# Heads' buffers, tied blocks, an early table load and layer 1's order on POOL and ACT: a two-layer kernel on one Trainium2 core

## The chip, the core and the metric

The kernel runs on one core of a Trainium2 chip. The core has five engines that run side by side, each in the order of its own queue: PE multiplies matrices (its weight loads are shown apart as PEld), DVE (VectorE) and ACT (ScalarE) work on elements, POOL (GpSimd) does slower element work, and SP (SyncE) here issues the DMAs, 16 DMA engines moving the data. On-chip memory has 128 partitions; sums of matmuls lie in the banks of PSUM, everything else in SBUF. Matmul operands of type fp32r are made in pairs, a high part and the low remainder, and three matmuls replace one exact product.

The metric is device time in microseconds (us), the median of several runs. A profile shows one execution. Its times run from the start of its span. A value in the form `out<-in` names the tiles by the program's names.

## The reference, cut

Two layers run over x of shape (4, 512, 1024). Each layer is an attention part and a feed-forward part, both on a layer-normalised x, both added to x.

```python
x = L0_attn_x
x = x + _L0_attn_ref(_layernorm(x, axis=-1))
x = x + _L0_ffn_ref(_layernorm(x, axis=-1), L0_ffn_W_base, ...)
x = x + _L1_attn_ref(_layernorm(x, axis=-1), L1_attn_wq_a, ...)
x = x + _L1_ffn_ref(_layernorm(x, axis=-1), L1_ffn_W, ...)
...
# _L1_attn_ref: 32 heads, 512 positions, causal
scores = jnp.einsum('bqhd,bkhd->bhqk', q_full, k_full) * softmax_scale
scores = jnp.where(causal[None, None], scores, jnp.finfo(scores.dtype).min)
attn = jax.nn.softmax(scores, axis=-1)
out = jnp.einsum('bhqk,bkhd->bqhd', attn, v).reshape(B, S, H * VD)
return out @ wo.T
...
# _L1_ffn_ref
q = x_q.mean(axis=1)                      # positions 179 to 510
routing = jax.nn.softmax(q @ router_W.T + router_b, axis=-1)
base = x @ W.T + b
t = jnp.einsum('bsd,erd->bser', x, A)
lora = jnp.einsum('bser,eor,be->bso', t, B, routing) * SCALING
return base + lora
```

The change lies in the second layer alone.

## The kernel before

The rows of x are 16 tiles of 128, four per batch. The second layer's attention runs in three stages.

*Projections* (`project`, `keep`, pools named `c1_...`). Tile after tile, PE sums the query and key projections into the bank `pq` (three banks), ACT takes the squares and the square root of the norm, and scales `qn`. PE transposes into `pn` (two banks), from there ACT and DVE write `qT` and `kT` in two halves, and SP stores them in DRAM (`q_d`, `kT_d`, `kF_d`, `k_d`). Beside the last tiles, `query` makes the queries of heads 0 and 1 in the bank `po` of pool `c1_pw`; `rotate_query` (ACT copies to `qf`, DVE makes `t`, POOL multiplies and adds) and `split_query` (DVE `qh`, POOL `ql`) follow.

*Heads* (pools `c2_...`). The units are group g of eight heads, batch b, head i. For each unit `scores` makes four rows of scores in the two banks of `pss`; for each row a custom DVE instruction (L874) adds the causal mask, writes `p` and takes the minimum, and ACT's Exp (L877) makes it probabilities. `turn` transposes p through `pst` (L898, copies at L900), `context` (L914) multiplies by v, and `divisors` sends the reciprocals of the sums through DRAM (`r_d`, then `rb`, one buffer) to the other partitions. `query` for unit u + 2 goes through the one bank `psq`. Fillers run between: `prepare_output` makes a group's output weights from `woT` and `wv` (`fetch_output` loads them into `slotC`) in eight blocks of two matmuls (`block`, L1022), each followed by ACT copies (`kept`, `high`) and DVE subtractions (`low`, `less`); `project` at L963 multiplies a finished batch by them and adds it to x in the tiles `xs` (pool `c2_x`, five buffers), loaded from and stored to `x_d` in DRAM. In these stages the order of each engine is made by a scheduler from priorities and its own estimate of times; `tc.issue_after(ins)` holds work back behind an instruction in that order. A pool stacks its tiles in memory where a closed pool's lay, so that a first write waits for the last use of what lay there, stores included.

*Layer 1's feed-forward part* (from `manual_schedule` on: PE, DVE, ACT and POOL keep the order of the program text; SP's order is the scheduler's). First the last batch's projection, 14 steps over two pairs of tiles; `fetch_last(j)` loads its four `xs` of the pair that starts at tile j. Then eight pairs of tiles, q = 0 to 7. Each pair is made in seven products (`STEPS`: b11, t1, t2, b22, t3, b21, t4), each in two halves s of the weights, with operands `ah` (ACT) and `al` (POOL) that are split ahead in three buffers. Weights come by `load_w1`: halves `wb`, `wt` or in the slots A, B, C; the kinds b11, b22 and b21 are partly split on the chip by `split_w1`. `product(q, step, s)` issues 12 matmuls and DVE adds the bank to the pair's tile (L1464; named `xo` for odd q, `raw` for even q). POOL adds the bias a quarter tile at a time (`biased`, L1442). Once per batch the routing is computed (`mixture`); `weighed` goes on in three moves through `go_on`: DVE weighs the LoRA inputs, then PE transposes them and ACT copies `hwh`, then DVE makes `hwl`; `lora` then multiplies and adds. `norm(q + 1, t)` normalises the next pair's tile t on ACT with `off` from `scales` on DVE, and `turn1` transposes it. `hs` holds these tiles; `wk` (`d_work`) holds small ones.

The pair's small tiles of LoRA are those of pair q - 1: for odd q, `weighed` is begun at step 2, copied at the end of step 3 and finished in step 4, where `lora(q - 1, 0)` follows; for even q it runs in steps 0 and 1. Pairs 2b and 2b + 1 belong to batch b, and the routing of a batch is computed at step 6 of its even pair, when the odd pair's tiles have been transposed. So an odd q has `lora` of the even pair of its own batch, an even q from 2 on (`behind`) that of the odd pair of the batch before.

The line that matters most for the wait at the junction:

```python
to = p[:, OF[i] : OF[i] + n]
turn_of[0] = V.tensor_tensor_reduce(out=to, in0=ps[:, 0:n], in1=causal[:, S - n : S], scale=1.0,
```

Of the kernel before, what the change touches and what calls it, by code (L numbers as in the profile page):

```python
# [46 lines left out]
def block_kernel(ctx: ExitStack, tc: tile.TileContext, a: dict, out: bass.AP):  # L47
# [662 lines left out]
    with tc.tile_pool(name="c1_w", bufs=1, side="right") as wap, \  # L710
            tc.tile_pool(name="c1_work", bufs=2) as wk, \
            tc.tile_pool(name="c1_pt", bufs=2, space=PSUM) as ptp, \
            tc.tile_pool(name="c1_pq", bufs=3, space=PSUM) as pqp, \
            tc.tile_pool(name="c1_pn", bufs=2, space=PSUM) as pnp, \
            tc.tile_pool(name="c1_pw", bufs=1, space=PSUM) as pwp:
        for ch in range(1, ND):
            split_shared(wap, ch)

# [9 lines left out]
        def project(s, hts):  # L728
            hh, hl = hts
            pq = pqp.tile([P, NA], F32, name="pq")  # L730
            for ch in range(ND):
                matmul3(pq, hh[:, ch, :], hl[:, ch, :], wA[ch][0], wA[ch][1],
                        start=(ch == 0), stop=(ch == ND - 1))
            j = order1[s] % TPB
            ss = small.tile([P, 2], F32, name="ss")
            junk = wk.tile([P, QR], F32, name="junk")
            A.activation(junk, pq[:, 0:QR], AF.Square, scale=QR ** -0.5, accum_out=ss[:, 0:1])
            A.activation(junk[:, 0:KVR], pq[:, QR : QR + KVR], AF.Square, scale=KVR ** -0.5,
                         accum_out=ss[:, 1:2])
            rs = rsqrt(ss, 2, 1e-6)  # L740
            qn = wk.tile([P, QR], F32, name="qn")
            kf = wk.tile([P, P], F32, name="kf")
            A.mul(qn, pq[:, 0:QR], rs[:, 0:1])
            V.scalar_tensor_tensor(out=kf[:, 0:KVR], in0=pq[:, QR : QR + KVR],
                                   scalar=rs[:, 1:2], in1=kvlnw, op0=ALU.mult, op1=ALU.mult)
            pe = QR + KVR
            half = ROPE // 2
            t1 = wk.tile([P, ROPE], F32, name="kt1")
            V.tensor_tensor(t1, pq[:, pe : pe + ROPE], ropeN[:, 0, j, :], ALU.mult)
            t2 = wk.tile([P, ROPE], F32, name="kt2")  # L750
            V.tensor_tensor(t2[:, 0:half], pq[:, pe + half : pe + ROPE],
                            ropeN[:, 1, j, 0:half], ALU.mult)
            V.tensor_tensor(t2[:, half:ROPE], pq[:, pe : pe + half],
                            ropeN[:, 1, j, half:ROPE], ALU.mult)
            V.tensor_tensor(kf[:, KVR:P], t1, t2, ALU.add)
            return qn, kf
# [22 lines left out]
                A.copy(kF, pn[:, 2, :])  # L779
                nc.sync.dma_start(out=kF_d[b], in_=kF)  # L780

        hts, qk = hts1, {}
        stats1[TPB - 1] = statistics([x[:, t, :] for t in order[-NB:]], "c", 4)
        for s in range(NT + 1):
            if s < NT:
                qk[s] = project(s, hts[s])
            if s + 2 < NT:
                hts[s + 2] = turn1(s + 2, ptp)
            if s > 0:
                keep(s - 1, qk[s - 1])  # L790
                if order1[s - 1] == TPB - 1:
                    batches[0, 0] = load_batch(0, 0)
            if s in (6, 10):
                wq_raw = fetch_query(s // 4 - 1)
            if s in (8, 12):
                wqs[s // 4 - 2] = prepare_query(wq_raw, pwp)
            if s in (NT - 2, NT - 1):
                query(s - NT + 2, pwp, "po")
                rotate_query(s - NT + 2)
            if s == NT - 1:  # L800
                split_query(0)
    c1.close()
    xpool.__exit__(None, None, None)

# [2 lines left out]
    with ExitStack() as c2:  # L807
# [3 lines left out]
        pso = c2.enter_context(tc.tile_pool(name="c2_pso", bufs=1, space=PSUM, side="right"))  # L811
        heads = c2.enter_context(ExitStack())
        tp = heads.enter_context(tc.tile_pool(name="c2_t", bufs=3))
        pp = heads.enter_context(tc.tile_pool(name="c2_p", bufs=2))
        rdp = heads.enter_context(tc.tile_pool(name="c2_rd", bufs=1))
        rdd = heads.enter_context(tc.tile_pool(name="c2_rdd", bufs=4, space=DRAM))
# [4 lines left out]

        OF = {3: 0, 2: 512, 1: 896, 0: 1152}

        sums_of = [None]

        turn_of = [None]
# [6 lines left out]
        def divisors(u, rs2):  # L833


            ri = turned_in[u // 2 % 2]
            V.reciprocal(ri[:, 0 : 2 * TPB], rs2.rearrange("p h i -> p (h i)"))
            rt = rdp.tile([P, 32], F32, name="rt")
            V.transpose(rt, ri)
            r_d = rdd.tile([2, TPB, P], F32, name="r_d")  # L840
            for k in range(P // 32):
                at = slice(k * 32, (k + 1) * 32)
                nc.sync.dma_start(out=r_d[:, :, at].rearrange("h i t -> (h i) t"),
                                  in_=rt[k * 32 : k * 32 + 2 * TPB, :])
            rb = divided[u - 1] = rdp.tile([P, S], F32, name="rb")
            for k in range(2):
                nc.sync.dma_start(out=rb[k * KVR : (k + 1) * KVR, :],
                                  in_=r_d[k].rearrange("i t -> (i t)").partition_broadcast(KVR))
# [4 lines left out]
        def scores(u):  # L853
# [10 lines left out]
            for i in range(TPB - 1, -1, -1):  # L864
                n = (i + 1) * P
                ps = pss.tile([P, S], F32, name="pss")
                if i == 0:
                    T.matmul(ps[:, 0:n], lhsT=f[:, 0:P], rhs=kF, start=True, stop=True)
                else:
                    at = slice((i - 1) * P, i * P)  # L870
                    matmul3(ps[:, 0:n], h[:, at], l[:, at], kT[:, 0, 0:n], kT[:, 1, 0:n],
                            start=True, stop=True)
                to = p[:, OF[i] : OF[i] + n]
                turn_of[0] = V.tensor_tensor_reduce(out=to, in0=ps[:, 0:n], in1=causal[:, S - n : S], scale=1.0,  # L874
                                                    scalar=-NEG, op0=ALU.add, op1=ALU.min,
                                                    accum_out=mn[:, i : i + 1])
                A.activation(to, to, AF.Exp, bias=mn[:, i : i + 1], scale=-1.0,  # L877
                             accum_out=rs[:, i : i + 1])
                if i > 0:
                    yield  # L880
# [126 lines left out]
        def prepare_output(g, fetched):  # L1007
# [9 lines left out]
            def block(n, half, at):  # L1017
                nonlocal fetched
                wo, wv = fetched
                po[at] = pso.tile([P, 512], F32, name="po" + at)  # L1020
                for k in range(2):
                    T.matmul(po[at][k * KVR : (k + 1) * KVR, :], lhsT=wv[:, k, :],  # L1022
                             rhs=wo[k][:, half * 512 : half * 512 + 512], start=True, stop=True)
                if half and n + 1 < len(prs):
                    fetched = fetch_output(g, prs[n + 1])

# [199 lines left out]
        abp = dp.enter_context(tc.tile_pool(name="d_a", bufs=1))  # L1226
        splits = dp.enter_context(tc.tile_pool(name="d_split", bufs=3))
        ptp = dp.enter_context(tc.tile_pool(name="d_pt", bufs=2, space=PSUM))
        NP = NT // 2
        blocks, sums, roots, offs = {}, {}, {}, {}  # L1230

# [77 lines left out]
        def fetch_last(j):  # L1309
            for t, k in ((0, 0), (1, 1), (0, 1), (1, 0)):  # L1310
                at[j + t, k] = x_d[(NB - 1) * TPB + j + t][k]
                xs[j + t, k] = xsp.tile([P, 512], F32, name="xs")
                nc.sync.dma_start(out=xs[j + t, k], in_=at[j + t, k])

        fetch_last(0)
# [4 lines left out]
        for n in range(14):  # L1320
# [36 lines left out]
                pair_sums(n - 10)  # L1357
            if n in (11, 12):
                parts.append(next(ops))
    w1p += [dp.enter_context(tc.tile_pool(name="d_w1", bufs=1, side="right"))]  # L1360
    hp = dp.enter_context(tc.tile_pool(name="d_h", bufs=1))
    w1r = dp.enter_context(tc.tile_pool(name="d_c", bufs=1, side="right"))
    xop = dp.enter_context(tc.tile_pool(name="d_x", bufs=1, side="right"))
    wk = dp.enter_context(tc.tile_pool(name="d_work", bufs=2, side="right"))
    acc = dp.enter_context(tc.tile_pool(name="d_acc", bufs=1, space=PSUM))
    lop = dp.enter_context(tc.tile_pool(name="d_lo", bufs=2, space=PSUM))
    for kind in ("b11", "b22", "b21", "t1"):
# [109 lines left out]
    for step in range(7):  # L1477
# [2 lines left out]
            split_w1("b11", 1, ((0, 1), (2, 3))[step - 3], V)  # L1480
        if step > 4:
            split_w1("b22", 1, (step - 5,), V)
    mix, at_work = None, {}

    def go_on(*keys):
# [3 lines left out]
    for q in range(NP):  # L1489
# [4 lines left out]
        for step in range(7):  # L1494
# [24 lines left out]
            if more and q + 1 >= TPB // 2:  # L1519
# [8 lines left out]
                    mv, r = root(mv, 2)  # L1528
                if step == 3:
                    scales(mv, r, 2, range(2 * q + 2, 2 * q + 4))  # L1530
            if more and step in (3, 4):
                norm(q + 1, step - 3)
            if q and 1 <= step < 5:
                for n in (0, 1):
                    biased(q, 2 * step - 2 + n)
            if q == 1 and step < 4:
                for n in (0, 1):
                    biased(0, 2 * step + n)
            if q:
                product(q, step, 0, h, l)  # L1540

            if (odd and step == 4) or (behind and step == 1):
                go_on((q - 1, 0), (q - 1, 1))
            if not more and step in (5, 6):
                go_on((q, step - 5))
# [3 lines left out]
            product(q, step, 1, h, l)  # L1549
            if not more and step == 6:  # L1550
                last_out(q, 1)

            if odd and step == 0:
                next(mix)
            if (odd and step == 3) or (behind and step == 0):
                go_on((q - 1, 0), (q - 1, 1))
            if odd and step in (4, 5):
                lora(q - 1, step - 4)
            if behind and step in (1, 2):
# [101 lines left out]
```

## Time and profile before

| | |
|---|---|
| median of three runs | 1771.49 us (1770.39 to 1771.75) |
| the profiled execution's own time | 1767.69 us |
| its span | 1765.9 us, granted clock 0.997 |
| PE busy | 1716.9 us, 97% of the span |
| DVE, ACT, POOL busy | 1312.4, 901.0, 892.3 us |
| chain that ended last | PE 84%, DVE 7%, DMA 3%, ACT 2% |
| projections end, heads begin | near 423 us |
| layer 1's feed-forward part begins | near 1508 us |

PE stands on most of the chain. In a timeline row, the first number is the start in us, the second the time during which such instructions ran, then come engine, line, operation and tiles; `xN` merges N instructions, and brackets hold the idle time of the engine just before and what ended it. In a table of windows, the columns are the window, its length, the busy us of each engine with the number of instructions, the granted clock of PE (1.00 is full), the mean busy share of the DMA engines and the rate at which they moved data.

### The profile page before, as it was taken

What the parts mean: (1) busy time and instruction counts of PE and PEld (TensorE: products, weight loads), DVE (VectorE), ACT (ScalarE), POOL (GpSimd) and SP (SyncE); (2) the same over time, 40 slices, a digit from 0 to 9 for tenths busy, and PEclk for the clock granted to TensorE, in tenths of its full rate; (3) what the DMA queues carried; (4) which work ended last, traced back from release to release, by engine and by line L of the source; (5) the groups of instructions that cost most, each with busy time, mean ns of one, the idle gap of its engine ahead of it and who ended that gap; (6) DMA issues with size and microseconds to landing.
All of it is one profiled execution on the core that took longest, in us unless ns stands there. A gap on an engine that the chain in (4) does not pass through costs nothing.

```text
span 1765.9 us, 31582 instructions
## 1 busy us (share of the span) xinstructions
PE 1716.9 (97%) x10536; PEld 1432.9 (81%) x10536; DVE 1312.4 (74%) x3517; ACT 901.0 (51%) x2315; POOL 892.3 (51%) x902
## 2 busy tenths in 40 slices
PE   6999999998999999999999999999999999989999
PEld 6999999997667777767777767777767777789998
DVE  6977885776877777787777687777778777677685
ACT  7422231465765555575555575555565555443332
POOL 0553540202556565546566546566545664665554
PEclk9999999999999999999999999999999999999999
DMA  4313553345224234343333353342454233943431
GB/s 192 134 50 123 169 169 98 99 136 177 81 92 148 80 113 142 114 167 112 109 114 120 108 189 93 103 139 93 135 176 138 98 117 117 328 153 127 142 110 61
DMA packets 131939, 228.16 MB, mean 129 GB/s; under 512 B 22272, under 2 KB 58752, under 8 KB 128448
## 3 DMA queue, kind: packets, MB, share of 16 engines
q1 hardware_dynamic: 131776, 226.13, 38.1%
q8 instruction: 84, 1.38, 0.3%
q14 instruction: 79, 0.65, 0.1%
HBM read 156.60 MB, written 71.83 MB: 129 GB/s over the span
## 4 chain that ended last, share of the span: by engine, by line
PE 84%; DVE 7%; DMA 3%; ACT 2%; POOL 1%; issue 1%; SPq 0%; DVEq 0%; POOLq 0%; ACTq 0%
PE psv L914 9%; PE pst L898 7%; PE pss L143 4%; PE po L143 4%; PE po L145 4%; PE po L144 4%; PE pss L144 4%; PE pss L145 4%; PE pob L143 3%; PE poa L143 3%; PE psq L143 3%; PE psq L145 3%; PE psq L144 3%; PE pob L145 3%; PE pob L144 3%; PE poa L144 3%
## 5 line engine op out<-in xcount | busy, mean ns | idle before, releaser
L877 ACT ACTIVATE p<-p,mn 128x512 f32<-128x512 f32 (+3 forms) x512 | 284.4, 559 | 206.2 <-DVE mn L874 206.0
L697 POOL TENSOR_TENSOR qf<-qf,ropeT 64x512 f32<-64x512 f32 x128 | 165.3, 1291 | 275.8 <-ACT qf L693 274.7
L874 DVE CUSTOM_DVE_ANT_0 p<-pss,causal 128x512 f32<-128x512 f32 (+3 forms) x512 | 231.4, 486 | 32.6 <-PE pss L145 25.0
L698 POOL TENSOR_TENSOR qf<-qf,t 64x512 f32<-64x512 f32 x128 | 165.7, 1294 | 40.8 <-DVE t L696 33.0
L898 PE MATMUL pst<-ident,p 128*128 128x128 f32 x1280 | 185.1, 273 | 0.7 <-ACT pT L900 0.7
L898 PEld LDWEIGHTS pst<-ident,p 128*128 128x128 f32 x1280 | 152.9, 141 | 25.5 <-ACT pT L900 2.4
L900 ACT COPY pT<-pst 128x512 f32<-128x512 f32 x256 | 141.7, 580 | 47.8 <-PE pst L898 46.9
L706 POOL TENSOR_TENSOR ql<-qf,qh 128x384 fp32r<-128x384 f32 x128 | 129.9, 1014 | 67.0 <-DVE qh L705 64.9
L143 PE MATMUL pss<-kT,ql 128*128 128x512 f32 (+2 forms) x384 | 144.5, 376 | 4.3 <-DVE mn L874 1.6
L949 POOL TENSOR_TENSOR cxl<-s,cxh 128x256 fp32r<-128x256 f32 x128 | 96.9, 765 | 89.5 <-ACT cxh L948 61.2
L143 PE MATMUL po<-w_h,hTl 128*128 128x384 f32 (+1 forms) x384 | 133.0, 346 | 0.2 <-DVE x L398 0.2
L144 PE MATMUL pss<-kT,qh 128*128 128x512 f32 (+2 forms) x384 | 130.8, 341 | 0.0
L145 PE MATMUL pss<-kT,qh 128*128 128x512 f32 (+2 forms) x384 | 130.2, 339 | 0.0
L145 PE MATMUL po<-w_h,hTh 128*128 128x384 f32 (+1 forms) x384 | 130.1, 339 | 0.0
L144 PE MATMUL po<-w_l,hTh 128*128 128x384 f32 (+1 forms) x384 | 129.7, 338 | 0.0
L900 DVE COPY pT<-pst 128x256 f32<-128x256 f32 x128 | 54.0, 422 | 95.8 <-PE pst L898 95.4
L693 ACT COPY qf<-psq 128x512 f32<-128x512 f32 x126 | 73.9, 586 | 71.0 <-PE psq L145 70.1
L695 DVE TENSOR_TENSOR t<-psq,ropeT 32x512 f32<-32x512 f32 x126 | 87.7, 696 | 24.2 <-ACT qf L693 20.2
L143 PEld LDWEIGHTS pss<-kT,ql 128*128 128x128 f32 x384 | 72.4, 189 | 39.4 <-POOL ql L706 11.4
L877 ACT ACTIVATION_READ_ACCUMULATOR p<-p,mn 128x1 f32 x512 | 97.3, 190 | 0.0
L696 DVE TENSOR_TENSOR t<-psq,ropeT 32x512 f32<-32x512 f32 x126 | 87.1, 691 | 1.8
L991 DVE TENSOR_TENSOR xs<-xs,pob 128x512 f32<-128x512 f32 x105 | 71.2, 678 | 19.7 <-PE pob L145 19.6
(563 smaller groups left out, 4963.8 us busy)
## 6 DMA issues: line engine op xcount, KB each, us to landing
xs<-x_d SPq DMA_DIRECT2D x128, 256.0 KB
x_d<-xs SPq DMA_DIRECT2D x128, 256.0 KB
slotC<-in_woT_dram SPq DMA_DIRECT2D x32, 512.0 KB
rb<-r_d SPq DMA_DIRECT2D x128, 128.0 KB
w_t<-raw SPq DMA_DIRECT2D x32, 288.0 KB
x<-in_x_dram SPq DMA_DIRECT2D x16, 512.0 KB
x_d<-x SPq DMA_DIRECT2D x32, 256.0 KB
slotA<-q_d SPq DMA_DIRECT2D x8, 1024.0 KB
```

The costliest lines, as they stand in the source:

```text
L143: T.matmul(ps, lhsT=al, rhs=bh, start=start, stop=False, **kw)
L144: T.matmul(ps, lhsT=ah, rhs=bl, start=False, stop=False, **kw)
L145: T.matmul(ps, lhsT=ah, rhs=bh, start=False, stop=stop, **kw)
L697: G.tensor_tensor(f[mid], f[mid], ropeT[mid, 0, :], ALU.mult)
L698: G.tensor_tensor(f[mid], f[mid], t2[mid], ALU.add)
L706: G.tensor_tensor(l, f[:, P:S], f32(h), ALU.subtract)
L874: turn_of[0] = V.tensor_tensor_reduce(out=to, in0=ps[:, 0:n], in1=causal[:, S - n : S], scale=1.0, scalar=-NEG, op0=ALU.add, op1=ALU.min, ...
L877: A.activation(to, to, AF.Exp, bias=mn[:, i : i + 1], scale=-1.0, accum_out=rs[:, i : i + 1])
L898: T.transpose(ps[:, w : w + P], p[:, OF[i] + j * P : OF[i] + (j + 1) * P], ident)
L900: copy(pT[:, AT[js[0]] : AT[js[0]] + w], ps[:, 0:w])
L914: T.matmul(ps[n * KVR : (n + 1) * KVR, S - w : S], lhsT=k[:, j, :], rhs=pTs[u + n][:, AT[j] : AT[j] + w], start=(j == 0), stop=(j == TPB - 1))
L949: G.tensor_tensor(l, src, f32(h), ALU.subtract)
```

## The change

Seven edits:

1. In the projections' stage the order of the PSUM pools is changed: `c1_pw` comes ahead of `c1_pn`, and `c1_pq` last.
2. `rb` gets a pool of its own, `c2_rb`, ahead of the pool of `p`, so that `p` lies elsewhere.
3. After the last tile's scaling, ACT computes one Exp on the one-column tile `first`.
4. In group 0 the matmuls of `block` are issued behind the latest unit's last row of scores.
5. Three of the four `xs` of the last batch's first pair get a pool `d_xl`, closed after the 14 steps.
6. `d_work` is opened earlier, next to the second half of the weights.
7. In the pairs, the bias is added after the products whose sums it follows, by the table `BIASED`; in odd pairs `norm(q + 1, 0)` comes after the copy of `hwh`, and `hwl` ahead of step 4's first product.

The numbers of instructions on each engine stay, but for the one Exp. The order in SP's queue changes with it at two places: near the first blocks the loads of `slotC` come after issues of `r_d` and `rb`, and around the last batch the loads of `xs` move up, between the stores of the batch before, while the loads of `slotB` (t3) and of `wb` for b21 come later.

```diff
             tc.tile_pool(name="c1_pt", bufs=2, space=PSUM) as ptp, \
-            tc.tile_pool(name="c1_pq", bufs=3, space=PSUM) as pqp, \
+            tc.tile_pool(name="c1_pw", bufs=1, space=PSUM) as pwp, \
             tc.tile_pool(name="c1_pn", bufs=2, space=PSUM) as pnp, \
-            tc.tile_pool(name="c1_pw", bufs=1, space=PSUM) as pwp:
+            tc.tile_pool(name="c1_pq", bufs=3, space=PSUM) as pqp:
...
-            A.mul(qn, pq[:, 0:QR], rs[:, 0:1])
+            scaled[0] = A.mul(qn, pq[:, 0:QR], rs[:, 0:1])
...
             if s == NT - 1:
                 split_query(0)
+                with tc.issue_after(scaled[0].ins):
+                    A.activation(first, first, AF.Exp)
...
         tp = heads.enter_context(tc.tile_pool(name="c2_t", bufs=3))
+        rbp = heads.enter_context(tc.tile_pool(name="c2_rb", bufs=1))
         pp = heads.enter_context(tc.tile_pool(name="c2_p", bufs=2))
...
-            rb = divided[u - 1] = rdp.tile([P, S], F32, name="rb")
+            rb = divided[u - 1] = rbp.tile([P, S], F32, name="rb")
...
-                    T.matmul(ps[:, 0:n], lhsT=f[:, 0:P], rhs=kF, start=True, stop=True)
+                    scored[0] = T.matmul(ps[:, 0:n], lhsT=f[:, 0:P], rhs=kF, start=True, stop=True)
...
-                for k in range(2):
-                    T.matmul(po[at][k * KVR : (k + 1) * KVR, :], lhsT=wv[:, k, :],
-                             rhs=wo[k][:, half * 512 : half * 512 + 512], start=True, stop=True)
+                with ExitStack() if g else tc.issue_after(scored[0].ins):
+                    for k in range(2):
+                        T.matmul(po[at][k * KVR : (k + 1) * KVR, :], lhsT=wv[:, k, :],
+                                 rhs=wo[k][:, half * 512 : half * 512 + 512], start=True, stop=True)
...
+        xl = ExitStack()
+        xlp = xl.enter_context(tc.tile_pool(name="d_xl", bufs=3))
...
-                xs[j + t, k] = xsp.tile([P, 512], F32, name="xs")
+                xs[j + t, k] = (xsp if j or (t, k) == (1, 0) else xlp).tile([P, 512], F32, name="xs")
...
+    xl.close()
     w1p += [dp.enter_context(tc.tile_pool(name="d_w1", bufs=1, side="right"))]
+    wk = dp.enter_context(tc.tile_pool(name="d_work", bufs=2, side="right"))
     hp = dp.enter_context(tc.tile_pool(name="d_h", bufs=1))
     w1r = dp.enter_context(tc.tile_pool(name="d_c", bufs=1, side="right"))
     xop = dp.enter_context(tc.tile_pool(name="d_x", bufs=1, side="right"))
-    wk = dp.enter_context(tc.tile_pool(name="d_work", bufs=2, side="right"))
...
+    BIASED = {(q, step): [(q, n) for n in ns] for q in range(1, NP)
+              for step, ns in ((0, (0, 1)), (1, (4, 5)), (2, (6, 7)), (3, (2, 3)))}
+    for at, ns in (((0, 6), (0, 1)), ((1, 0), (2,)), ((1, 1), (3,)), ((1, 2), (4,)), ((1, 3), (5,)),
+                   ((1, 4), (6, 7))):
+        BIASED.setdefault(at, []).extend((0, n) for n in ns)
...
-            if more and step in (3, 4):
+            if odd and step == 4:
+                go_on((q - 1, 0), (q - 1, 1))
+            if more and step in ((4,) if odd else (3, 4)):
                 norm(q + 1, step - 3)
-            if q and 1 <= step < 5:
-                for n in (0, 1):
-                    biased(q, 2 * step - 2 + n)
-            if q == 1 and step < 4:
-                for n in (0, 1):
-                    biased(0, 2 * step + n)
             if q:
                 product(q, step, 0, h, l)
-            if (odd and step == 4) or (behind and step == 1):
+            if behind and step == 1:
                 go_on((q - 1, 0), (q - 1, 1))
...
             product(q, step, 1, h, l)
...
+            for p, n in BIASED.get((q, step), ()):
+                biased(p, n)
...
             if (odd and step == 3) or (behind and step == 0):
                 go_on((q - 1, 0), (q - 1, 1))
+            if odd and more and step == 3:
+                norm(q + 1, 0)
```

More of the change, by code (lines that the diff above doesn't have):

```diff
@@ L780, in keep @@
                 nc.sync.dma_start(out=kF_d[b], in_=kF)
-        hts, qk = hts1, {}
+        hts, qk, scaled = hts1, {}, [None]
         stats1[TPB - 1] = statistics([x[:, t, :] for t in order[-NB:]], "c", 4)
@@ L822, in block_kernel @@
         OF = {3: 0, 2: 512, 1: 896, 0: 1152}
+        scored = [None]
         sums_of = [None]
```

## The prediction

> **What bounds the kernel now.** I read the page first: PE is busy for 1716.9 us of a span of 1765.9, so only 49 us can be won at all unless PE work goes, and no PE work goes here. Then I cut the span into windows to see where those 49 us lie, and read the chain of waits, PE's waits and the timeline only there. Until 340 us PE idles 20 us, at the start, which no edit touches. The rest sits in a few places. The windows' columns are: window, length, then busy us and instructions of PE, its weight loads, DVE, ACT and POOL, the granted PE clock, the DMA share and GB/s.
>
> ```profile
> 420.00:430.00 10.00, 6.70 (x25) 3.10 (x23) 5.07 (x18) 4.32 (x11) 4.10 (x6) 0.85 0.87 279
> 430.00:440.00 10.00, 7.78 (x32) 5.84 (x32) 6.04 (x23) 7.65 (x21) 3.55 (x3) 0.81 0.50 166
> 440.00:450.00 10.00, 9.94 (x64) 7.79 (x65) 7.58 (x21) 5.84 (x16) 6.76 (x7) 1.00 0.09 27
> ...
> 1570.00:1580.00 10.00, 8.16 (x59) 7.50 (x57) 8.32 (x20) 1.89 (x4) 10.00 (x13) 1.00 0.01 2
> 1580.00:1590.00 10.00, 8.81 (x49) 7.80 (x50) 5.03 (x13) 4.23 (x8) 5.37 (x7) 0.83 0.26 96
> ```
>
> Here PE loses 5.5 us between 420 and 440 and 3.0 between 1570 and 1590, both times at a clock below 1: part of each window ran at half rate. (Between 1510 and 1570 it loses 5.3 more.) After 440 it is full. The timeline shows what it waits for at the first place, the change from projections to heads:
>
> ```profile
> 426.22 1.22 PE L1022 MATMUL poa<-slotC 128*64 128x512 f32 x4 [2.13 <-issue]
> ...
> 429.43 0.69 DVE L874 CUSTOM_DVE_ANT_0 p<-pss,causal 128x512 f32<-128x512 f32 x1 [3.31 <-DMA kT_d<-kT]
> 429.79 1.28 ACT L877 ACT_TABLE_LOAD   x1
> ...
> 440.06 0.50 PE L143 MATMUL pss<-kT,ql 128*128 128x512 f32 x1 [0.95 <-POOL ql L706]
> ```
>
> Bracketed is the idle time and what ended it. The first score row of head 0 has lain in its bank since 423.5, but DVE may not write `p` until the DMA store of the last `kT` has left that memory, at 429.4. ACT's exponentials then also wait for a table load. PE waits for the bank of `poa`, then for both score banks, at last for the third head's rotated query. The second place is layer 1's pairs with odd q:
>
> ```profile
> 1576.10 0.46 DVE L1464 TENSOR_TENSOR xo<-xo,acc 128x288 f32<-128x288 f32 x1 [1.43 <-POOL xo L1442]
> ...
> 1579.42 1.24 ACT L1266 ACTIVATE h<-h,off,y2d 128x1024 f32<-128x1024 f32 x1 [4.30 <-DVE off L1258]
> ...
> 1580.57 0.41 ACT L1432 CAST hwh<-pt 128x128 fp32r<-128x128 f32 x2
> ...
> 1581.19 0.80 PE L143 MATMUL lo<-b1h,hwl 128*128 128x512 f32 x1 [2.72 <-DVE hwl L1434]
> ...
> 1638.40 0.50 PE L143 MATMUL lo<-b1h,hwl 128*128 128x512 f32 x1 [1.14 <-DVE hwl L1434]
> ```
>
> The LoRA copy `hwh` stands on ACT behind the norm, the norm waits for `off`, and in q=1 `off` is late because a sum waited 1.43 us for POOL's bias. Lastly one wait hangs on the loads:
>
> ```profile
> 1553.76 0.38 PE L143 MATMUL acc<-wt,al 128*128 128x288 f32 x1 [1.63 <-DMA wt<-w_t]
> ```
>
> **The change, part by part. Junction at 420 to 440 (PSUM pools reordered, `rb` moved ahead of `p`, Exp loaded early, blocks tied).** In the changed program DVE's first L874 waits for PE and DVE alone. It stands behind the query scaling, which ends at 425.15 + 0.35 = 425.5 and doesn't move: ACT's table load moves into the idle 1.72 us that end at 423.37 (ACT is free from 421.65; 1.28 + 0.3 for a one-column Exp ends at 423.2). So `p` starts at 425.6, 3.8 earlier. If that cover were gone, the load would cost its 1.28 again. Follow the third head's query: four exponentials at 0.72, 0.60, 0.49, 0.39, with 0.19 each for the accumulator, end at 429.4 (from 426.4); `qf` copied at 430.0 (0.57); L695 and L696, 0.70 each, at 431.4; POOL L698 1.28 at 432.7; `qh` 0.36, `ql` 1.00 at 434.15. PE may go on at 434.2, where it did at 440.06: 5.9 earlier. The 3.8 became 5.9 because the load (1.28) and three copies of block results (1.76) no longer stand on ACT ahead of the exponentials. PE, however, owes the eight block matmuls that it did in its wait, 1.01 per four by the later rows of L1022, 2.0. I take 5.9 - 2.0 = 3.8 (rounded down). Ends: 5.9 if the owed matmuls fall into waits that remain, 2.0 if the three copies come back on the path. The tie adds a wait that PE meets anyway: blocks now stand behind head 3's scores, behind them queries and transposes. On SP the next `slotC` loads (two of 512 KB, one of 64) fall behind the `r_d` and `rb` issues; PE meets the block that needs them some 7 us of its own work later, against 2.43 and 4.11 us that the chain shows for single loads (`xs`, `raw`).
>
> [...]
>
> **LoRA copies before the norm, bias behind sums.** In q=1 the sum at 1576.10 loses its 1.43. DVE's `off` then ends near 1577.95 and step 3's sums at 1580.18 - 1.43 = 1578.75. `hwh` is copied once the transposes (1574.12 + 0.38) are there, and `hwl` now comes ahead of step 4's sums: 1579.0. PE, free at 1578.47, waits 0.6 in place of 2.72. The six LoRA matmuls cost 0.43 each at half rate against 0.23; their eight transposes then end at 1581.6, held a little by the second norm (1577.98 + 1.24 + 0.62 + 1.25), where they ended at 1585.07: 3.5. Ends: 2.1 (half rate stays), 4.0 (no wait left). For q=3 and q=5 nothing waits for POOL; `hwl` leaves the place behind the norm: DVE ends step 3's sums at 1637.39, `hwl` 0.26 later, PE starts at 1637.72 for 1638.40; the second norm takes back 0.1. Twice 0.6 is 1.2, ends 0.4 and 2.3.
>
> [...]
>
> POOL pays nothing: a bias is 0.72, a split 1.28, a step of 24 matmuls at 0.133 is 3.2. The bias now waits for DVE's sum, some 0.8 behind PE, and the next split stands behind it: 0.8 + 3 x 0.72 + 1.28 = 4.3, while that split is due two steps, 6.4, later. Beyond this margin each us would be PE's.
>
> **Last batch and small tiles.** Three `xs` buffers leave the pool of five, so loads of `x_d` no longer wait for stores. On SP four loads move up between the stores at 1505 to 1509, the other half's three also; `slotB` slides from 1503.54 behind them, and `wb` (b21, 1.18 MB) from 1511.96 behind all the `raw` loads to about 1522.5. What DVE gains (1.44 at 1526.60) hides behind POOL, busy without a break there. But the loads behind that `wb` are those that end in the 1.63. 1.18 MB at the 385 to 424 GB/s of full windows is 3.0 us, 0.65 less for the 256 KB load that left: 2.4 late at worst; of it the DMA's slack between 1520 and 1526 (shares 0.57, 0.81, 0.90 of 2 us each) takes 1.4. I take a loss of 1.0. Ends: a gain of 1.6, a loss of 2.4 and 1.3 for half rate after a 4-us gap. `d_work` moved: nothing, its first tile is written at 1536.96 after DVE idled 2.67 for PE, and `bias`, whose memory shifts, is used 28 us after its issue.
>
> **Sum.** 3.8 + 3.5 + 1.2 - 1.0 = 7.5. The profiled execution took 1767.69, 3.8 under the median of 1771.49; I apply the saving to both: 1760.2 and 1764.0.
>
> **Rivals.** (1) The junction only moves its wait: the third head's query, by way of POOL, stays where it was. Only layer 1's 3.7 remain: 1767.8. For it: that wait is a chain through four engines. Against: all of it hangs on `p`, and the new order shows no DMA there. (2) Loads decide: the b21 move costs 3.7 and the junction brings 2.0, together 3.0 saved, 1768.5. For: the DMA share is about 1.0 from 1526 to 1556. Against: the same bytes move. (3) Slower: the tied blocks become the bound. First to last block took 62 us; the first now comes near 445, 18 us later, while the first projection stays at 507 less the lead. If the block-copy-subtract chain needed all of its 62, PE would wait 18 there: 1771.5 - 7.5 + 18 = 1782; it decides once it slips by more than 7.5. Against: a block's own chain is about 3.1 us (0.5 matmul, two copies of 0.59, two subtractions of 0.69), eight are 25.
>
> **Chances.** Forecast 0.69 (its own range 1761 to 1767), rivals 0.12, 0.15 and 0.04. About 0.2%, 3.5 us, is what a measurement of this kernel tells from no change. Faster takes nearly all of the first and half of (1) and (2): 0.80; the same 0.16; slower 0.04. The terms' ends alone give 1757.7 and 1770.7; 1759.5 to 1770 leaves out under two in ten.
>
> **What would show it.** Right: L874 starts near 425.6 with no DMA as releaser, ACT's load stands before L770, PE's first wait for `ql` ends near 434; PE's waits for `hwl` fall from 5.8 to about 2.3, with the clock at 1.0 in the window after q=1. Wrong: a wait of `poa` or `pob` for `slotC` or DVE between 440 and 510, or a `wt` wait well above 1.63.

## The result, and the profile after

| | before | after |
|---|---|---|
| median | 1771.52 us (1770.39 to 1771.99, 6 runs) | 1759.94 us (1757.68 to 1762.22, 6 runs) |
| ratio, 95% interval | | 0.994 (0.9929 to 0.995) |
| the profiled execution, and its span | 1767.69, 1765.9 us | 1762.22, 1760.4 us |
| PE busy | 1716.9 us | 1714.4 us |

The kernel got faster by 11.6 us. The forecast was 7.5, 1764.0: the direction holds, and the size is half as large again. The time lies 1.1 us below the forecast's own range of 1761 to 1767 and only 0.4 us inside the wider one of 1759.5 to 1770. The two profiled executions differ by only 5.5 us, since the one of before is 3.8 under its median and the one of after 2.3 over its own. That gap is the first thing to explain.

Some windows of the profile after (window, length, then busy us and instructions of PE, its weight loads, DVE, ACT, POOL, the granted clock, DMA share, GB/s):

```profile
420.00:430.00 10.00, 7.65 (x32) 5.57 (x31) 6.91 (x27) 7.47 (x24) 5.06 (x7) 0.87 0.94 291
430.00:440.00 10.00, 9.34 (x46) 8.15 (x45) 7.07 (x20) 5.96 (x16) 5.93 (x5) 0.78 0.24 79
...
1580.00:1590.00 10.00, 10.00 (x75) 9.60 (x74) 5.28 (x11) 3.40 (x7) 5.15 (x6) 1.00 0.67 217
...
1630.00:1640.00 10.00, 10.00 (x70) 9.47 (x69) 6.81 (x19) 5.02 (x9) 5.28 (x5) 1.00 0.31 104
```

Between 420 and 440 PE idles 3.0 us in place of 5.5, yet the clock is as low as before: in this execution the half-rate stretch stayed (6.83 us from 427.48 on, 6.83 from 427.03 on in before). The windows behind q = 1 and in q = 3 are full, and the clock there is 1. The timeline of after at the junction and in q = 1:

```profile
423.06 1.28 ACT L804 ACT_TABLE_LOAD   x1
...
426.83 0.68 DVE L882 CUSTOM_DVE_ANT_0 p<-pss,causal 128x512 f32<-128x512 f32 x1
...
436.76 0.50 PE L143 MATMUL pss<-kT,ql 128*128 128x512 f32 x1 [0.66 <-POOL ql L706]
...
1574.14 0.42 ACT L1445 CAST hwh<-pt 128x128 fp32r<-128x128 f32 x2
...
1577.20 1.24 ACT L1277 ACTIVATE h<-h,off,y2d 128x1024 f32<-128x1024 f32 x1 [2.64 <-DVE off L1269]
...
1578.22 0.50 PE L143 MATMUL lo<-b1h,hwl 128*128 128x512 f32 x1 [0.87 <-DVE hwl L1447]
```

`p` no longer waits for a DMA, the table load stands ahead of it, and PE's wait for `hwl` in q = 1 fell from 2.72 to 0.87, with `hwh` copied 3 us ahead of the norm.

**How the traces are compared below.** The n-th instruction of a form (DVE's rows of scores, its sums, its reciprocals) is the same piece of work in both kernels. Its lead is how much earlier it starts than in the first profile of before; what a stretch is worth is the growth of the lead over it. Leads in us, at the time that the instruction has in the profile of before:

| profile | 420 | 538 | 1507 | 1561 | 1567 | 1607 | 1719 |
|---|---|---|---|---|---|---|---|
| after | -1.40 | 3.28 | 2.27 | 1.70 | 0.87 | 3.73 | 5.45 |
| e1, edits 1 to 4 | 0.10 | 7.19 | 6.68 | 4.63 | 4.63 | 5.98 | 5.72 |
| e2, edit 7 | -0.17 | -0.10 | -1.90 | -4.59 | -5.42 | -2.54 | -0.71 |
| e3, edits 5, 6 | 1.21 | 1.17 | 0.73 | -4.45 | -4.47 | -4.49 | -4.82 |
| e4, before again | 0.45 | 0.33 | -0.44 | -3.15 | -3.14 | -3.35 | -3.31 |
| e5, after again | 0.01 | 7.00 | 6.46 | 3.85 | 3.02 | 5.91 | 7.64 |
| e6, without 5, 6 | 0.50 | 7.14 | 6.30 | 2.68 | 1.85 | 4.73 | 6.49 |
| e7, edits 2, 5, 6 | 1.21 | 7.65 | 6.56 | 3.54 | 3.55 | 4.90 | 4.89 |
| e8, LoRA first | 0.23 | 1.78 | 1.37 | -1.87 | -1.86 | 0.19 | 1.48 |
| e9, bias moved | -0.18 | 5.36 | 4.01 | 3.37 | 3.44 | 6.21 | 7.93 |
| e10, without 3 | 1.17 | 7.22 | 6.54 | 3.48 | 2.64 | 5.54 | 7.26 |
| e11, without 4 | 1.53 | 6.23 | 5.84 | 5.42 | 4.60 | 7.50 | 9.22 |
| e12, edits 2, 7 | 1.06 | 8.26 | 7.82 | 6.33 | 6.41 | 9.24 | 11.03 |

Where a run's table of times gives a ratio, it is against the kernel before on the same chip.

### The profile page after: what moved, and what is told of

It is laid out like the page before. It is cut to its first block, busy times and chain, and to the rows that moved or that the text cites. A ratio compares the mean times of both kernels' runs of the same rounds, so it can differ in the third digit from the quotient of the medians.

```text
span 1760.4 us, 31605 instructions
## 1 busy us (share of the span) xinstructions
PE 1714.4 (97%) x10536; PEld 1433.1 (81%) x10536; DVE 1311.9 (75%) x3517; ACT 901.5 (51%) x2316; POOL 895.7 (51%) x902
## 4 chain that ended last, share of the span: by engine, by line
PE 87%; DVE 6%; DMA 3%; ACT 2%; POOL 1%; issue 1%; SPq 0%; DVEq 0%; ACTq 0%; POOLq 0%
PE psv L922 9%; PE pst L906 7%; PE po L143 4%; PE po L145 4%; PE po L144 4%; PE pss L143 4%; PE pss L144 4%; PE pss L145 4%; PE poa L143 3%; PE pob L143 3%; PE psq L143 3%; PE psq L145 3%; PE psq L144 3%; PE poa L145 3%; PE poa L144 3%; PE pob L145 3%
```

## The experiments

**The parts alone, and the kernel before again.** e1 has edits 1 to 4 of the diff, e2 edit 7, e3 edits 5 and 6, each on the kernel before; e4 is the kernel before, unchanged.

> Edits 1 to 4 alone (pool orders, the buffer of the reciprocals, the early Exp, tied blocks). By the two profiled executions the lead grows from -1.4 at 420 us to 3.3 at 510 us: 4.7 saved, so the median falls from 1771.5 to about 1766.8 (theory A: the parts add, each as large as in the traces). Theory B (the two traces miss a part, because the half-rate stretch after 427 us comes in some executions only): 7 to 8 saved, 1763.5 to 1764.5, with executions whose mean clock is 0.999 or 1.000 beside others at 0.998. My prediction's rival 1 (the wait only moves) would have 0 saved: 1771.5.

> Edit 7 alone (bias behind sums, LoRA copies ahead of the norm). By the traces q=1 saves 2.9 to 3.4 us, q=3 and q=5 0.86 each: 4.6 to 5.1 saved, 1766.4 to 1766.9 (theory A, and B too). Theory C (edit 7 counts only with the earlier loads of edits 5 and 6): under 3 saved, above 1768.5.

> Edits 5 and 6 alone (three buffers of xs apart, the small tiles' pool moved). By the traces the lead shrinks by 1.4 us between 1510 and 1567: 1.4 slower, about 1772.9 (theory A: the loads that were moved back cost this). Theory C: no loss or a small gain alone, 1770.5 to 1771.5. PE's wait for wt would be near 2.1 by A, 1.6 or less by C.

> The kernel before, once more, unchanged. Its one profiled execution took 1767.69, 3.8 under the median. Theory A: this profile was a lucky one; the new profile and the executions lie at 1770.5 to 1772, and their extra 3 to 4 us can be found in the trace in a stretch outside the edits (start to 420 us, or the heads). Theory B: the executions split into two groups by the mean clock (0.996 and 0.997 or more), and the new profile has a longer half-rate stretch near 427 or 1580 us than 7 and 5 us.

| | median, range, runs | ratio, 95% interval |
|---|---|---|
| kernel before | 1769.48 (1765.83 to 1772.59, 31) | |
| e1, edits 1 to 4 | 1762.56 (1761.21 to 1767.82, 8) | 0.9965 (0.9954 to 0.9976) |
| e2, edit 7 | 1765.20 (1763.27 to 1770.25, 12) | 0.9981 (0.9971 to 0.9991) |
| e3, edits 5, 6 | 1772.60 (1771.26 to 1774.69, 11) | 1.002 (1.0011 to 1.0028) |
| e4, before again | 1769.54 (1767.18 to 1774.05, 11) | 1.0002 (0.9993 to 1.0011) |

Edits 1 to 4 bring 6.9 us (by the interval 4.2 to 8.1), more than theory A's 4.7 and just short of B's 7 to 8. Edit 7 brings 4.3 (1.6 to 5.1), near A's 4.6. The interval alone leaves room for C, but the lead grows by 3.9 from 1561 to 1719 in e2 and by 3.8 in after, so edit 7 needs no other edit. Edits 5 and 6 alone cost 3.1 (1.9 to 5.0), twice what A had, and C's gain is out; edit 6 was never run without edit 5. The spread of the kernel before, some 7 us, is as large as what is sought, so the traces have to carry the rest. They show why it is so wide. Windows of two profiles in which the junction's code is the one of before (first e8, then e4):

```profile
430.00:440.00 10.00, 7.62 (x42) 5.86 (x41) 7.00 (x23) 6.51 (x21) 5.24 (x5) 1.00 0.43 157
```

```profile
430.00:440.00 10.00, 7.95 (x35) 6.28 (x35) 6.41 (x20) 6.69 (x20) 4.53 (x4) 0.83 0.41 155
1510.00:1520.00 10.00, 7.74 (x32) 6.28 (x31) 4.63 (x12) 6.23 (x10) 3.14 (x5) 0.83 0.83 292
```

The same waits at the junction are followed by half rate in e4 and by none in e8, whose lead grows by 1.55 from 420 to 538 with no edit in it (its window from 420 to 430 has a clock of 1.00 too). e4 has a stretch near 1517 that the first profile of before lacks. Theory B is right in this: the half-rate stretches come in some executions only. It is wrong in its groups, since times and clocks spread without two clear clusters. Theory A is right that the profile of before was a lucky one, but the place is not where A looked (before 420 us, or the heads); it is 1507 to 1561. With the loads in the order of before, six other profiles (e1, e2, e4, e6, e8, e12) lose 1.5 to 3.6 us there against it. That accounts for most of the 3.8 us to the median. Half rate is not all of it: in e2 and e12, which lose 2.7 and 1.5 there, the clock is 1.00 from 1507 to 1561, and PE's wait for `wt` is 2.7 and 2.5 us in place of 1.63.

**Why edits 5 and 6 alone lose.** SP's queue, the first sum of the last batch on DVE and PE's wait behind it in e3, by the timeline:

```profile
1504.40 4.63 SPq L995 DMA_DIRECT2D x_d<-xs  x4
1509.19 3.20 SPq L1315 DMA_DIRECT2D xs<-x_d  x7
...
1512.11 0.69 DVE L1336 TENSOR_TENSOR xs<-xs,poa 128x512 f32<-128x512 f32 x1 [3.43 <-issue]
...
1512.94 0.47 PE L143 MATMUL poa<-t20h,cxl 128*128 128x512 f32 x1 [2.43 <-DVE y L1253]
```

And SP's queue in after:

```profile
1502.88 0.33 SPq L1003 DMA_DIRECT2D x_d<-xs  x1
1503.25 0.43 SPq L1324 DMA_DIRECT2D xs<-x_d  x1
1504.25 0.32 SPq L1003 DMA_DIRECT2D x_d<-xs  x1
1504.61 0.43 SPq L1324 DMA_DIRECT2D xs<-x_d  x1
```

In e3 seven loads stand in one block behind four stores. DVE idles 3.4 us before the sum that adds to one of the loaded tiles (the view names no releaser, "issue"; the first load is issued 2.9 us before the sum starts). PE idles 2.4 until that sum has emptied the bank (the view names `y`, DVE's next instruction), after which its clock halves: matmuls on 128x512 go from 0.39 to 0.63 us. In after the loads stand between the stores. Theory D explains it by the memory that the new buffers get: without edit 2 the first of them lies where a late tile of the heads' stage lay, with `rb` in its own pool ahead of `p` it doesn't. No row shows where a tile lies, so this reason stays argued; that edits 5 and 6 hang on edit 2 can be tested.

**The full change again, without edits 5 and 6, edits 2, 5 and 6 alone, and half of edit 7.** e6 leaves out `d_xl` and the move of `d_work`. e7 takes only these and `rb`:

```diff
+        rbp = heads.enter_context(tc.tile_pool(name="c2_rb", bufs=1))
         pp = heads.enter_context(tc.tile_pool(name="c2_p", bufs=2))
...
-            rb = divided[u - 1] = rdp.tile([P, S], F32, name="rb")
+            rb = divided[u - 1] = rbp.tile([P, S], F32, name="rb")
```

e8 changes the kernel before in the pairs' order alone; the bias stays where it was:

```diff
-            if more and step in (3, 4):
+            if odd and step == 4:
+                go_on((q - 1, 0), (q - 1, 1))
+            if more and step in ((4,) if odd else (3, 4)):
                 norm(q + 1, step - 3)
...
-            if (odd and step == 4) or (behind and step == 1):
+            if behind and step == 1:
                 go_on((q - 1, 0), (q - 1, 1))
...
+            if odd and more and step == 3:
+                norm(q + 1, 0)
```

> The changed kernel once more. Against the kernel before on this chip, the three parts measured alone gave -6.9 (edits 1 to 4), -4.3 (edit 7) and +3.1 (edits 5 and 6). Theory A (parts add): -8.1, 1761.4 if the kernel before stands at 1769.5. Theory D (edits 5 and 6 cost 3.1 only where the loads of xs stand behind four stores in SP's queue; in the full change they stand between them, since edit 2 frees the memory they go to): -10.5 to -11.5, 1758 to 1759. The share of executions with clock 0.999 or 1.000 above that of the kernel before in both.

> The changed kernel without edits 5 and 6. Theory A: 3.1 faster than the full change, -11.2 against the kernel before, 1758.3. Theory D: equal to the full change within 1 us either way.

> Edits 2, 5 and 6 alone, so that the loads of xs can stand between the stores. Theory D: between 1500 and 1530 us the lead changes by less than 0.5, where edits 5 and 6 alone lost 3.2, and DVE's first sum of the last batch no longer idles 3.4; PE's wait there falls from 2.4 to 1.2 or less. Theory A: 3 lost there as before. The junction may gain or not: edit 2 moves p away from the memory of kT, so up to 4.7 saved there; if the PSUM order alone decides, 0. Time 1765 to 1770 by D, 1768 to 1773 by A.

> Half of edit 7: LoRA copies and hwl ahead of the norm, the bias where it was before. My prediction's steps: q=3 and q=5 keep their whole saving (0.6 each forecast, 0.9 measured), in q=1 PE's wait for hwl goes from 2.7 to about 1 although the sum still waits 1.43 for POOL's bias: 3.0 to 4.3 saved in all, 1765.2 to 1766.5 at 1769.5 for the kernel before. Rival: the late bias holds hwl too, because hwl stands on DVE behind the sums of step 3: only 1.8 from q=3 and q=5, 1767.7, and q=1 keeps a wait of 2 or more.

| | median, range, runs | ratio, 95% interval |
|---|---|---|
| kernel before | 1769.39 (1765.92 to 1772.03, 17) | |
| e5, the full change | 1759.10 (1755.87 to 1762.23, 6) | 0.9939 (0.9925 to 0.9953) |
| e6, without edits 5, 6 | 1758.38 (1756.44 to 1761.19, 6) | 0.9937 (0.9924 to 0.995) |
| e7, edits 2, 5, 6 | 1761.81 (1760.39 to 1764.52, 5) | 0.9956 (0.9943 to 0.997) |
| e8, LoRA first | 1767.32 (1766.18 to 1769.26, 12) | 0.9992 (0.9983 to 1.0) |

e5 and e6 are equal within the scatter, 10.3 and 11.0 saved. D had 10.5 to 11.5 for e5; A's 8.1 lies just outside its interval (8.3 to 13.3 saved), while e6 alone fits A's 11.2 as well as D. The traces decide. In e7 SP's loads stand between the stores, the lead between 1507 and 1528 shrinks by 0.14, where e3 lost 3.2, and PE waits 1.3 there for 2.4: edits 5 and 6 cost nothing there once edit 2 is in, as D says. What nobody expected is the junction in e7: 6.4 us from one moved buffer, without the other three edits.

In e8 half of edit 7 brings 2.1 us, less than the 3.0 that my step asked for. The timeline of its q = 1:

```profile
1576.89 0.43 ACT L1432 CAST hwh<-pt 128x128 fp32r<-128x128 f32 x2
...
1577.95 0.45 DVE L1464 TENSOR_TENSOR xo<-xo,acc 128x288 f32<-128x288 f32 x1 [1.43 <-POOL xo L1442]
...
1581.96 0.47 DVE L1434 TENSOR_TENSOR hwl<-pt,hwh 128x128 fp32r<-128x128 f32 x2
...
1582.30 0.51 PE L143 MATMUL lo<-b1h,hwl 128*128 128x512 f32 x1 [1.97 <-DVE hwl L1434]
```

`hwh` is there at 1577.3, but DVE stands 1.43 for POOL's bias, then makes `off`, then the sums of step 3, and only then `hwl`; PE still waits 1.97. The rival was right: in q = 1 the new order of LoRA and norm is not enough without the later bias. The later bias without the new order was not run. In q = 3 and 5, e8 keeps 1.3 of the 1.7 to 1.8 that e2 and e5 have.

**The last four: one loss mended, edits 3 and 4 undone, and the smallest version.** e9 differs from the full change in one number, e10 lacks the early Exp, e11 the tie of the blocks, and e12 has edits 2 and 7 alone, with the number of e9:

```diff
-    for at, ns in (((0, 6), (0, 1)), ((1, 0), (2,)), ((1, 1), (3,)), ((1, 2), (4,)), ((1, 3), (5,)),
+    for at, ns in (((0, 4), (0, 1)), ((1, 0), (2,)), ((1, 1), (3,)), ((1, 2), (4,)), ((1, 3), (5,)),
```

> The full change, with the first two bias additions for pair 0 put after step 4 of q = 0 where the change has them after step 6. Theory E (after step 6 they run on POOL beside two DVE operations on the path to the routing: b1l took 0.98 and s 1.22 us there, 0.68 each without POOL, together 0.84): the lead over the kernel before no longer shrinks by 0.83 between 1561 and 1567 us, b1l and s take 0.7 each, and the time falls by 0.8 against the full change, to about 1758.3 if that stands at 1759.1. Rival: the two additions take the same from DVE or delay the next split elsewhere, and the lead at 1570 is no larger than in the full change.

> The full change without edit 3. My prediction's step: the table load stands again ahead of head 0's first exponential and costs its 1.28 on the path; the lead won between 420 and 540 us falls from 7.0 (clock full) or 4.7 (with a half-rate stretch) by 1.3, the time rises to about 1760.4. Rival (edit 2 alone won 6.4 with the load in that place): the load is covered, 0.3 or less is lost, 1759.4 or less.

> The full change without edit 4. My prediction's step: the first blocks come early, their three copies (1.76 us on ACT) come ahead of exponentials, and the third head's query is later by up to 1.76, though PE no longer owes 2.0 later: between 0.2 faster and 1.8 slower, 1759 to 1761. Rival: with p free early, the blocks fall into the waits left at the junction and their copies into ACT's gaps, so that the kernel gets faster by up to 1: 1758.

> Edits 2 and 7 alone, with the two additions after step 4. If edit 2 holds nearly all of the junction (6.4 of 7.0) and edits 5 and 6 are worth nothing in the median, as edits 1 to 4 and 7 without them were (1758.4 beside 1759.1): 1757.9 to 1759.5, no slower than the full change. Rival: edits 1, 3, 4, 5 and 6 together are worth 2 or more: above 1760.5.

| | median, range, runs | ratio, 95% interval |
|---|---|---|
| kernel before | 1770.12 (1766.08 to 1776.34, 11) | |
| e9, bias after step 4 | 1758.20 (1757.12 to 1761.25, 6) | 0.9931 (0.9915 to 0.9947) |
| e10, without edit 3 | 1759.55 (1757.69 to 1763.53, 6) | 0.9939 (0.9922 to 0.9957) |
| e11, without edit 4 | 1761.21 (1758.41 to 1762.86, 6) | 0.9949 (0.9932 to 0.9966) |
| e12, edits 2, 7 | 1760.72 (1756.63 to 1762.09, 6) | 0.9938 (0.9921 to 0.9956) |

The four times overlap, and only the traces tell the kernels apart. Theory E first. DVE and POOL near the routing of batch 0, in before, in after and in e9:

```profile
1564.02 0.68 DVE L1579 TENSOR_TENSOR b1l<-raw,b1h 128x512 fp32r<-128x512 f32 x1
1564.62 0.68 DVE L940 TENSOR_TENSOR s<-s,a 128x512 f32<-128x512 f32 x1
```

```profile
1562.02 1.86 POOL L1455 TENSOR_TENSOR raw<-raw,bias 128x256 f32<-128x256 f32 x2
...
1562.32 0.98 DVE L1599 TENSOR_TENSOR b1l<-raw,b1h 128x512 fp32r<-128x512 f32 x1
1563.22 1.22 DVE L948 TENSOR_TENSOR s<-s,a 128x512 f32<-128x512 f32 x1
```

```profile
1551.39 1.43 POOL L1455 TENSOR_TENSOR raw<-raw,bias 128x256 f32<-128x256 f32 x2
...
1560.65 0.68 DVE L1599 TENSOR_TENSOR b1l<-raw,b1h 128x512 fp32r<-128x512 f32 x1
1561.25 0.69 DVE L948 TENSOR_TENSOR s<-s,a 128x512 f32<-128x512 f32 x1
```

Two additions on POOL, which took the two DVE operations from 0.68 to 0.98 and 1.22 us, stood in after beside the chain that ends in the next operand. The lead falls by 0.83 between 1561 and 1567 in every profile that has the bias there (after, e2, e5, e6, e10, e11: 0.82 to 0.84) and by none in the others (e9 and e12: grows by 0.07 and 0.08). E is shown; the price of edit 7 at this place is 0.83, and one number takes it back. The rows lengthen on both engines at once: POOL's two additions take 1.86 us there and 1.43 in e9. Why they do was not shown.

Now the junction. ACT in e10, then ACT in e11, then DVE and PE in e12:

```profile
425.02 1.28 ACT L882 ACT_TABLE_LOAD   x1 [0.38 <-DVE mn L879]
426.32 0.72 ACT L882 ACTIVATE p<-p,mn 128x512 f32<-128x512 f32 x1
```

```profile
423.40 0.59 ACT L1037 COPY raw<-poa 128x512 f32<-128x512 f32 x1 [0.75 <-DMA k_d<-kf]
...
425.71 0.59 ACT L1037 COPY raw<-pob 128x512 f32<-128x512 f32 x1 [0.29 <-PE pob L1028]
426.19 0.72 ACT L883 ACTIVATE p<-p,mn 128x512 f32<-128x512 f32 x1
```

```profile
422.54 0.69 DVE L877 CUSTOM_DVE_ANT_0 p<-pss,causal 128x512 f32<-128x512 f32 x1 [0.17 <-PE pss L145]
...
429.15 1.08 PE L1025 MATMUL poa<-slotC 128*64 128x512 f32 x4
...
433.07 0.50 PE L143 MATMUL pss<-kT,ql 128*128 128x512 f32 x1 [0.17 <-POOL ql L706]
```

Growth of the lead from 420 to 538, where no half-rate stretch fell: full edits 1 to 4 7.0 (e5), 7.1 (e1), 6.6 (e6); without the early Exp 6.05 (e10), so the load in its old place costs 0.6 to 1.0 (by 445 us the growth is 5.0 for 5.9), which lies between the step's 1.28 and the rival's 0.3; without the tie 4.70 (e11), 1.9 to 2.4 less. Of this 1.2 is lost by 445 us (4.7 for 5.9): there the copies of blocks stand ahead of the first exponentials on ACT, as the prediction's lower end had it. The rest comes later, and the section on the prediction shows where. Yet edit 2 alone has 7.2 (e12). There `p` starts at 423.6 on the clock of before (422.54 and its lead of 1.06), ahead of the last query scaling, the table load still stands behind it, and a first group of block matmuls fills PE's wait, so that the third head's query costs PE 0.17 in place of 0.97 us in e5. Edits 1, 3 and 4 together bring nothing on top of edit 2 in these traces; none of the three was run on edit 2 by itself. In e11 (edits 1 to 3) the first blocks stand ahead of the scores, in e7 and e12 behind them; so edit 1 or 3 brings them forward, and the tie pushes them back.

e12's profile is the shortest of all (a span of 1754.9), its median is 1.6 us over that of e5, on another chip; it has the loads in the order of before. Its rival, above 1760.5, has the median just on its side. Six executions don't settle this: its interval holds the ratios of e5, e6 and e9. No version measured here is faster than the full change beyond the intervals. For e9 the trace gives 0.8 us.

## Why the prediction was right, and what it mis-sized

**The junction's start: right.** `p` was to start at 425.6 and PE's wait for the third head's query to end at 434.2. e5, whose lead at 420 is 0.01, so that its times can be read against before, has:

```profile
425.42 0.68 DVE L882 CUSTOM_DVE_ANT_0 p<-pss,causal 128x512 f32<-128x512 f32 x1
...
433.94 0.50 PE L143 MATMUL pss<-kT,ql 128*128 128x512 f32 x1 [0.97 <-POOL ql L706]
```

Rival 1 (the wait only moves) is out. So is rival 3: between 440 and 520 `poa` waits 0.2 us for `slotC` in after and `pob` 0.9 for DVE's sum of `xs`, near 510, where before had 0.8 idle as well. One reason given was off: the step from 3.8 to 5.9 is not ACT's alone. ACT's first exponential starts at 426.20 in e5 for 431.08 in before, 0.9 more than `p` gains; another 1.2 comes from DVE, which makes the third head's `t` behind two of the second head's rows (429.59) and in before behind all four (435.71).

**The junction's sum: mis-sized, and this is the step that failed.** "5.9 - 2.0 = 3.8" became 4.7 (after) and 5.5 (e9) with a half-rate stretch, 6.6 to 7.1 without. The growth of the lead shows the terms. By 445 us it is 5.9 in e1, e5 and e6, as forecast, and 4.0 (after) and 5.1 (e9) behind a stretch. The eight owed block matmuls then take back 1.6 in each of the five by 454, somewhat less than the 2.0. What the sum lacked comes after that: from 454 to 505 the lead grows again by 2.1 to 2.8. For the same matmuls in another order (but for a few at the ends) the PE of before takes 51.7 us there, that of e5 49.0. Of the difference rows show 0.5 as idle time. Another 1.6 lies in the order itself, by two rows of before:

```profile
455.33 1.07 PE L1022 MATMUL poa<-slotC 128*64 128x512 f32 x2
...
468.14 1.08 PE L1022 MATMUL poa<-slotC 128*64 128x512 f32 x4
```

Two matmuls of this form alone took 1.07 us here, four in a row 1.08. From start to next start, the 82 matmuls with 64 columns (`po` from `slotC`, and `psv`) take 19.1 us in before, where six pairs stand alone, and 17.5 in e5. In e11 they take 19.1 as well and the whole stretch 51.8: it has none of the 2.7, though it owes no 1.6 either. Some 0.6 of the 2.7 stays open.

The sum also had nothing for a half-rate stretch that comes or stays away. The profiles with the junction of before had it four times in five; those with some of edits 1 to 4 three times in nine. The mean clock was 0.999 or more in 4 of 8 executions of e1, and in 4 of 31 of the kernel before beside it. That fits a stretch that comes less often behind shorter waits, but it is too few to be called shown. The mean growth of the five profiles with all four edits is 6.2, that of the five without any 0.3: 5.9 us.

**Layer 1: right in mechanism.** LoRA was to start on PE at 1579.0 and its eight transposes to end at 1581.6. In after they do at 1578.22 and 1580.81, with the lead of 0.87 at 1579.1 and 1581.7. The saving in q = 1 was 3.5; it is 3.4 at 1592 and 2.9 from 1607 on. Part of it is again the clock. The forecast had half rate hang on the length of the wait, a term that no run shows: e1 and e7, with the order of before and its wait of 2.7, had no half-rate stretch behind it and gained 1.35 by that alone. For q = 3 and 5 the 1.2 is 1.7, since PE's wait for `hwl` is gone there. In all, PE's waits for `hwl` fell from 5.8 to 2.4 us, where 2.3 was forecast. "POOL pays nothing" was wrong: the additions didn't delay POOL, but DVE beside it, by 0.83. I had looked at POOL's time alone, and not at what runs on DVE meanwhile.

**The loads: a loss of 1.0 that isn't there.** From 1507 to 1561 the profiles with the changed queue (after, e5, e7, e9, e10, e11) lose 0.4 to 3.1 against the first profile of before, 1.7 in the mean; those with the old queue (before, e1, e2, e4, e6, e8, e12) 0 to 3.6, 2.3 in the mean. PE's wait at the half of `wt` that hangs on the loads is 1.4 to 2.7 with the old queue and 0.9 to 2.9 with the new (there put down to `al` or `wb` twice). So the move of b21's `wb` costs nothing that can be seen, and rival 2 is out. No run shows the 1.3 for half rate after a 4-us gap either: the longest of these waits is 2.9. The wait in after is 2.15, above the 1.63 that was to be a sign of being wrong; but that base came from the execution that loses least of the seven.

**The sum.** By the leads: 5.9 + 2.4 (q = 1, 2.86 less the mean of 0.5 that profiles of the old order gain by chance) + 1.7 - 0.8 + 0.5 = 9.7, beside 10.3 and 11.6 in the two comparisons of medians and 7.5 in the forecast. 2.1 of the missing 2.2 stand at the junction. The other misses (-1.1 in q = 1, +0.5 in q = 3 and 5, -0.8 on DVE beside POOL, +1.5 at the loads) cancel to 0.1, which is luck. The leads leave 0.6 to 1.9 us of the medians' gain unexplained.

## What to carry to other kernels

Where waits of 1 to 3 us are cut, look at several profiles of the kernel before: the place, not only the length, of the slow stretches differed here from one execution to the next (e4 has one near 1517 that the first profile lacks), and one profile can hide or feign some us (1.5 to 3.6 between 1507 and 1561 here). When pools are reordered, try the one move that removes the wait alone; other edits at the same place may only pay for one another. Follow the work on for some 50 us behind the place that was changed: here the new order of the fillers gave back more there, 2.1 to 2.8 us, than the 1.6 that the owed work had cost. When work moves on POOL, read the rows of DVE beside its new place (here 0.98 and 1.22 us for 0.68), not POOL's own slack.

## What the runs showed of the hardware

In these runs no one length of PE's idle time decided whether half rate followed. By the clock's records such a stretch lasted 6.83 us from 427.03 and 3.41 us from 1580.73 on in before, and 6.83 us from 427.48 on in after; three windows of 10 us in e4 have a clock of 0.83, which is 3.4 us at half rate in each. A wait of 2.7 us for `hwl` was followed by it in before and by none in e1 (the windows from 1570 to 1590 there have a clock of 1.00 throughout); in after it began at 427.48 with no single wait above 1.2 us, and in e5 the same program, with much the same waits (the longest 1.16), kept the full clock, 1.00 in both windows from 420 to 440.
